# A hybrid scan/attention block with routed experts: a launch with fewer loads, vector-engine norms, late constants, a first pair of batches, and three changes of order and places

## The chip, the cores and the metric

The kernel runs on one core of a Trainium2 chip. The core has a matrix engine (PE), a vector engine (DVE), a scalar engine (ACT), a general engine (POOL), and a sync engine (SP) that mostly issues DMA transfers. Each engine works through its own list of instructions in order and waits on semaphores where it needs another's result. The metric is device time in microseconds (us) of one execution; the number given is the median over the runs.

## The reference

The input x has 8 batches of 512 tokens of width 256, all in float32. Four steps follow each other, each adding to x: a scan layer, a mixture of experts, causal attention, and the same mixture of experts again.

```python
x = x + scan(layernorm(x))        # silu(x @ Win), h = 0.9*h + xt*Bp, y = h.Cp + Dp*xt, y @ Wout
x = x + ffn(layernorm(x))
x = x + attention(layernorm(x))   # 16 heads of width 16, causal, softmax, Wout
x = x + ffn(layernorm(x))
```

Since the scan's state is decayed by one constant and multiplied by Bp and Cp for each channel, the kernel scans one number per channel and multiplies by sum(Bp*Cp). The ffn is

```python
scores = sigmoid(x @ router_w.T)              # 16 experts in 4 groups, best 2 groups, best 4 experts
tw = scores of the 4 chosen / their sum * 2.5
routed = sum over the 4: tw * (silu(x@gate_w) * (x@up_w)) @ down_w
sh = silu(x @ sh_gate_w) * (x @ sh_up_w) @ sh_down_w       # shared experts, every token
return routed + sh
```

## The kernel before

A batch is a tile of 128 partitions by NT = 4 rows of 256 numbers. The program has four stretches of time. The **Scan stage** goes over the 8 batches; then the **routed experts** of the first ffn; then the **Attention stage** over the 8 batches; then the routed experts of the second ffn, beside which the sums of finished batches go to the output.

Inside a stage, `stretch` builds, for every batch b, a set of pieces (Python generators) and `beside` weaves them by how many matmul columns each piece has behind it: `timed(piece, at...)` puts the steps of a piece at given shares of the batch's main work. So the program's order is laid down when the kernel is built, and a scheduler keeps dependences by semaphores; `tc.keep_in_program_order` pins an instruction to the place where it was written, and `tc.issue_after` keeps it behind another one. In loop b of the Scan stage there run: the main work of batch b (`Scan.main`: four times a projection pz, a sigmoid on ACT, the product xi on DVE, the scan on DVE, a multiplication on ACT and the sum y on DVE, then the output projection py and its addition to x); the norm, transposes, logits and choice of experts of batch b-1 (`Route`); the sending of batch b-2's rows to the experts' lists (16 indirect DMAs on POOL, L665); the shared experts of batch b-2; and the loading, norm and transposes of batch b+1. In Scan `ahead` is 1, in Attention 2, where the first two batches are prepared beside the last routed blocks by `prepared`.

`normed` (L376) makes a layernorm: statistics by bn_stats and bn_aggr on DVE, 1/sqrt(var + eps) either by a DVE addition and a pow on POOL (L401, L402), or, with `by_vector`, by an integer first guess and three Newton steps on DVE; then four row normalisations on DVE (L405). For a routed batch its output is the tile sorted_m, of which the iota on POOL (L526) fills the token numbers. The gain write (L651) puts the four weights of each token into that tile; the tile is then sent by the DMAs of L665. The tag "rows" holds two such tiles.

`routed` (L765) works through 136 blocks of 128 rows. `load` (L792) brings a block's rows, in tag "kb4", on SP; `fetch` copies an expert's weights; `turn`, `up` and `down` do the matmuls; a scatter DMA on POOL (L859) adds the results to part 0. The shared experts' output ys_m goes to part 1 by SP (L948). There is a branch (L889, L892) ahead of the blocks for an unlikely overflow; each engine passes it. `load_sum` (L140) loads part 0 and part 1 of a batch and adds them on DVE at one go (L145). In Attention, L991 makes the queries and keys, which L999 to L1002 copy into masked places (`w_all`), half of it on ACT and half on DVE; L1046 makes the scores.

At the head of the program x_0 and x_1 go out on SP, the weights of Scan on ACT, the shared experts' weights sg, su and sd on SP and ACT, and small ones on POOL; the routing's constants (parity, mine, groups, cand_*, below) are made on DVE from the identity.

Of the kernel before, what the change touches and what calls it, by code (L numbers as in the profile page):

```python
# [15 lines left out]
P = 128  # L16
# [7 lines left out]
HG = 4  # L24
# [50 lines left out]
def tile_hybrid_block(  # L75
# [56 lines left out]
    def load_x(b: int):  # L132
        x_sb = xpool.tile([P, NT, D], FP, tag="x", name=f"x_{b}")
        x_tiles[b] = x_sb
        return nc.sync.dma_start(out=x_sb, in_=x_in[b].rearrange("(t p) d -> p t d", p=P))
# [4 lines left out]
    def load_sum(i: int, b: int, more, queue=nc.sync):  # L140

        x_sb = xpool.tile([P, NT, D], FP, tag="x", name=f"x{i}_{b}")
        queue.dma_start(out=x_sb, in_=rows_of(parts[i][0], b))
        queue.dma_start(out=more, in_=rows_of(parts[i][1], b))
        nc.vector.tensor_add(x_sb, x_sb, more)  # L145
        x_tiles[b] = x_sb

# [28 lines left out]

    sg_sb = const.tile([P, KD, NSH * F], FP, name="sg_sb")
    nc.sync.dma_start(out=sg_sb, in_=sh_gate_w.rearrange("(k p) f -> p k f", p=P))
    su_sb = const.tile([P, KD, NSH * F], FP, name="su_sb")
    nc.scalar.dma_start(out=su_sb, in_=sh_up_w.rearrange("(k p) f -> p k f", p=P))  # L180
    sd_sb = const.tile([P, NSH * KF, D], FP, name="sd_sb")
    nc.sync.dma_start(out=sd_sb, in_=sh_down_w.rearrange("(k p) d -> p k d", p=P))
# [32 lines left out]
    nc.gpsimd.memset(decay, DECAY)  # L215
# [3 lines left out]
    nc.vector.tensor_mul(bc_all, bp_sb, cp_sb)  # L219
    bc_sb = const.tile([P, NI], FP, name="bc_sb")  # L220
    nc.vector.tensor_reduce(bc_sb, bc_all, AX.X, ALU.add)

    def load_attention_weights():
# [9 lines left out]
    nc.vector.tensor_reduce(  # L233
        parity, ident.rearrange("p (q w c) -> p w q c", q=HG, w=2), AX.XY, ALU.add
# [29 lines left out]
    nc.vector.tensor_reduce(mine, ident.rearrange("p (g e) -> p e g", e=E), AX.X, ALU.add)  # L264
    groups = const.tile([P, P // E], FP, name="groups")
    nc.vector.tensor_reduce(groups, ident.rearrange("p (g e) -> p g e", e=E), AX.X, ALU.add)
    cand_e = const.tile([P, 1], FP, name="cand_e")
    spelled = const.tile([P, E], FP, name="spelled")
    nc.vector.tensor_mul(spelled, mine, numbers)
    nc.vector.tensor_reduce(cand_e, spelled, AX.X, ALU.add)  # L270
    cand_j = const.tile([P, CAND], FP, name="cand_j")
    nc.vector.tensor_mul(spelled[:, 0 : P // E], groups, numbers[:, 0 : P // E])
    nc.vector.tensor_reduce(cand_j[:, 0:1], spelled[:, 0 : P // E], AX.X, ALU.add)
    for c in range(1, CAND):
        nc.vector.tensor_scalar(cand_j[:, c : c + 1], cand_j[:, 0:1], float(c * (P // E)), None, ALU.add)
    below = const.tile([P, E], FP, name="below")
    nc.vector.tensor_scalar(below, numbers, cand_e, None, ALU.is_lt)
    cand_at = const.tile([P, 2, CAND], FP, name="cand_at")
    nc.vector.tensor_scalar(cand_at[:, 1, :], cand_j, float(BLK), None, ALU.mult)
    for c in range(CAND):  # L280
        nc.vector.tensor_scalar(cand_at[:, 0, c : c + 1], cand_e, float(WEXP), None, ALU.mult)
        nc.vector.scalar_tensor_tensor(
            cand_at[:, 1, c : c + 1], cand_e, float(REG), cand_at[:, 1, c : c + 1], ALU.mult, ALU.add
        )
# [91 lines left out]
    def normed(b: int, tag: str, place, by_vector: bool = False):  # L376

        x_sb = x_tiles[b]
        stats = small.tile([P, NT, 6], FP, tag="stats", name=f"stats_{tag}")
        mv = small.tile([P, NT, 2], FP, tag="mv", name=f"mv_{tag}")  # L380
        for t in range(NT):
            nc.vector.bn_stats(stats[:, t, :], x_sb[:, t, :])
            nc.vector.bn_aggr(mv[:, t, :], stats[:, t, :])
            yield
        rstd = small.tile([P, NT], FP, tag="rstd", name=f"rstd_{tag}")
        if by_vector:


            var = small.tile([P, NT], FP, tag="var", name=f"var_{tag}", bufs=1)
            nc.vector.tensor_scalar(var, mv[:, :, 1], EPS, None, ALU.add)  # L390
            bits = small.tile([P, NT], I32, tag="bits", name=f"bits_{tag}", bufs=1)
            nc.vector.tensor_scalar(bits, var.bitcast(I32), 1, None, ALU.logical_shift_right)
            nc.vector.tensor_scalar(rstd.bitcast(I32), bits, -1.0, HALVED, ALU.mult, ALU.add)
            off = small.tile([P, NT], FP, tag="off", name=f"off_{tag}", bufs=1)
            for _ in range(3):
                nc.vector.tensor_mul(off, rstd, rstd)
                nc.vector.scalar_tensor_tensor(off, off, -0.5, var, ALU.mult, ALU.mult)
                nc.vector.scalar_tensor_tensor(rstd, off, 1.5, rstd, ALU.add, ALU.mult)
            yield
        else:  # L400
            nc.vector.tensor_scalar(rstd, mv[:, :, 1], EPS, None, ALU.add)  # L401
            nc.gpsimd.tensor_tensor(rstd, rstd, neg_half, ALU.pow)  # L402
        xn = place()
        for t in range(NT):
            nc.vector.tensor_scalar(  # L405
                xn[:, t, :], x_sb[:, t, :], mv[:, t, 0:1], rstd[:, t : t + 1], ALU.subtract, ALU.mult
            )
            yield
# [24 lines left out]
    class Scan:  # L433
# [4 lines left out]
        norms, scores, choose = (0.08, 0.2, 0.32, 0.4), (0.48, 0.52, 0.61, 0.66), (0.71, 0.97)  # L438

# [72 lines left out]
    counts = [region, region]  # L512
    upto = {}

    class Route:
# [8 lines left out]
        def place(self):  # L524
            rows = work.tile([P, NT, ROW], FP, tag="rows", name=f"sorted_{self.tag}")
            nc.gpsimd.iota(  # L526
                rows[:, :, D + 2 * TK :].bitcast(I32), [[P, NT], [0, 8]], base=self.b * T, channel_multiplier=1
# [4 lines left out]
        def norm(self, by_vector: bool = False):  # L532
            return normed(self.b, self.tag, self.place, by_vector)
# [27 lines left out]
    def choices(i: int, b: int, tag: str, held, paced: bool):  # L561
# [89 lines left out]
        nc.vector.scalar_tensor_tensor(  # L651
# [113 lines left out]
    def routed(i: int, table, beside):  # L765
# [4 lines left out]
        held = {}  # L770
# [21 lines left out]
        def load(n: int):  # L792
            if n not in held:
                values(n)
            rows = work.tile([P, 4 * D], FP, tag="kb4", name=f"rows_{i}_{n}", bufs=KB)
# [73 lines left out]
        def run(first: int, last: int):  # L869
            load(first)  # L870
# [25 lines left out]
    def shared_experts(i: int, b: int, xnT_of, tanh: bool):  # L896
# [3 lines left out]
        def steps():  # L900
# [47 lines left out]
            nc.sync.dma_start(out=rows_of(parts[i][1], b), in_=y_sb)  # L948
# [15 lines left out]
    class Attention:  # L964
        mixture, ahead, copies = 1, 2, by_both
        early = 2
        norms, scores, choose = (0.0, 0.12, 0.2, 0.28), (0.42, 0.46, 0.55, 0.6), (0.66, 0.95)

# [4 lines left out]
        def load(self, b: int):  # L973
            load_sum(0, b, kb4(f"more0_{b}"))
# [157 lines left out]
    def prepared(b: int):  # L1132
# [17 lines left out]
        def begin():  # L1150
            x_sb = xpool.tile([P, NT, D], FP, tag="x", name=f"x0_{b}")
            more = free_home("v", f"more_{b}")
            for j, dst in ((1, more), (0, x_sb)):
                nc.gpsimd.dma_start(out=dst, in_=rows_of(parts[0][j], b))
            held.update(x=x_sb, more=more)

        def add():
            for t in range(0, NT, 2):
                rows = held["x"][:, t : t + 2, :]
                tc.keep_in_program_order(nc.vector.tensor_add(rows, rows, held["more"][:, t : t + 2, :]))  # L1160
            x_tiles[b] = held["x"]
# [30 lines left out]
    def stretch(layer):  # L1192
# [5 lines left out]
        def norm(b: int):  # L1198
# [4 lines left out]
            return normed(b, f"l{i}_{b}", place)  # L1203

        def turn(b: int):
            return turned(lambda: xn.pop(b), f"l{i}_{b}", lambda xnT: xT.update({b: xnT}), layer.copies)
# [11 lines left out]
        for b in range(layer.ahead):  # L1218
# [4 lines left out]
            else:  # L1223
                layer.load(b)
                issue(Piece(0, norm(b)))
                issue(Piece(0, turn(b)))
            if b == 0:
                issue(project(b))
        def start_route(b: int):
# [4 lines left out]
        for b in range(B):  # L1234
            pieces = [layer.main(b, made.pop(b))]
# [15 lines left out]
            if b > 0:  # L1251
                r = start_route(b - 1)
                if last:
                    pieces.append(timed(r.norm(), *spread(0.0, 0.12, NT), *spread(0.2, 0.28, NT)))
# [15 lines left out]
            if nxt < B:  # L1270
                layer.load(nxt)
# [5 lines left out]
            if layer.ahead == 1 and nxt < B:  # L1277
                issue(project(nxt))
        layer.end()
# [163 lines left out]
```

## Time and profile before

| | us |
|---|---|
| median of 3 runs (1785.84 to 1786.67) | 1786.35 |
| profiled execution | 1778.1 |
| its span | 1776.4 |

Where PE was busy in the profiled execution, from the busy time of each engine by stretch:

| stretch, us from the start | length | PE busy | DVE busy | PE clock granted |
|---|---|---|---|---|
| 0 to 20, launch | 20 | 3.95 | 8.59 | 1.00 |
| 20 to 60, first Scan batch | 40 | 32.77 | 33.32 | 0.91 |
| 60 to 120, Scan | 60 | 60.00 | 49.97 | 1.00 |
| 120 to 280, Scan | 160 | 151.80 | 115.10 | 1.00 |
| 280 to 320, end of Scan | 40 | 30.72 | 26.27 | 0.79 |
| 320 to 374, last shared experts | 54 | 48.19 | 23.03 | 0.99 |
| 374 to 780, routed experts | 406 | 405.04 | 231.23 | 0.99 |
| 780 to 800, start of Attention | 20 | 9.96 | 8.70 | 0.74 |
| 800 to 1350, Attention | 550 | 539.48 | 358.28 | 1.00 |
| 1350 to 1360, second routed start | 10 | 4.00 | 2.50 | 0.66 |
| 1360 to the end | 416.4 | 388.82 | 233.45 | 0.97 |

In these tables and in the profile's lines a matmul's busy time ends where the model of the pipeline ends it, "idle before" is the time in which the engine stood before an instruction, and the arrow names what ended that wait. SPq and POOLq are the queues of DMA-issuing instructions of SP and POOL. Batch starts in Scan are taken as the first pz matmul of a batch on PE: 63.87 (batch 2), 102.27 (3), 141.68 (4), 183.40 (5), and 264.82 (7).

### The profile page before, as it was taken

How to read it: one execution, taken by the hardware profiler on the slowest of the kernel's cores; microseconds unless marked ns; L12 is line 12 of the kernel's file. 1: busy time of each engine (PE TensorE's matmuls, PEld its weight loads, DVE VectorE, ACT ScalarE, POOL GpSimd, SP SyncE). 2: the span in 40 equal slices, each digit the busy share in tenths (PEclk: the TensorE clock that was granted, in tenths of full speed). 3: DMA queues.
4: the chain of work that ended last, by engine and by line, in shares of the span. 5: the costliest groups of instructions: out<-in, count | busy, mean ns of one | idle time of the engine just before them, and what ended most of it. 6: DMA issues, size and time to landing. Idle time of an engine off the chain costs nothing. (4 is left out here: it accounts for less than half of the span.)

```text
span 1776.4 us, 32812 instructions
## 1 busy us (share of the span) xinstructions
PE 1674.7 (94%) x10640; PEld 1253.8 (71%) x10640; DVE 1090.5 (61%) x3399; ACT 805.7 (45%) x1740; POOL 772.2 (43%) x675
## 2 busy tenths in 40 slices
PE   5999998989999999979999999999998999999994
PEld 3566664579999999954445455455466999999993
DVE  5977767435555655545776675766753665555552
ACT  2322222135555555535654554544523555555552
POOL 4255554625555655530021422312452555555663
PEclk9999998999999999989999999999999999999997
DMA  5443322535555655530012112112443555566766
GB/s 168 161 152 128 131 91 91 184 76 96 95 98 108 103 98 94 98 83 13 25 50 73 63 61 73 52 58 78 145 177 79 94 98 94 103 134 128 129 123 178
DMA packets 149998, 181.37 MB, mean 102 GB/s; under 512 B 16096, under 2 KB 136960, under 8 KB 149824
## 3 DMA queue, kind: packets, MB, share of 16 engines
q0 software_dynamic: 54432, 81.53, 24.1%
q1 hardware_dynamic: 93600, 93.50, 17.3%
q10 hardware_dynamic: 1792, 4.19, 0.6%
q8 instruction: 89, 1.46, 0.3%
q14 instruction: 85, 0.70, 0.1%
HBM read 81.62 MB, written 97.53 MB: 101 GB/s over the span
## 5 line engine op out<-in xcount | busy, mean ns | idle before, releaser
L859 POOL DMA_INDIRECT part<-rows x272 | 428.3, 1575 | 363.6 <-ACT rows L858 287.4
L665 POOL DMA_INDIRECT xg<-sorted_m,slots_m x256 | 256.5, 1002 | 279.4 <-ACT slots_m L662 115.5
L822 PEld LDWEIGHTS ph<-rows,gate 128*128 128x128 f32 x2176 | 285.9, 192 | 15.8 <-ACT rows L812 1.1
L822 PE MATMUL ph<-rows,gate 128*128 128x128 f32 x2176 | 289.3, 276 | 0.6 <-ACT rows L812 0.6
L822 PE MATMUL ph<-rows,up 128*128 128x128 f32 x2176 | 288.5, 276 | 0.0
L850 PE MATMUL pyr<-w_all,rows 128*128 x1088 | 280.4, 380 | 0.0
L822 PEld LDWEIGHTS ph<-rows,up 128*128 128x128 f32 x2176 | 266.0, 193 | 0.0
L830 ACT ACTIVATE rows<-ph 128x256 f32<-128x256 f32 x272 | 104.5, 384 | 328.7 <-PE ph L822 328.7
L831 DVE TENSOR_TENSOR rows<-ph,rows 128x256 f32<-128x256 f32 x272 | 115.3, 424 | 194.1 <-ACT rows L830 193.8
L850 PEld LDWEIGHTS pyr<-w_all,rows 128*128 128x128 f32 x1088 | 185.2, 191 | 14.2 <-ACT rows L858 0.4
L804 ACT COPY gate<-w_all 128x512 f32 x272 | 170.1, 627 | 14.7 <-SPq L892 2.5
L1057 ACT ACTIVATE w_all<-ps_a 128x1024 f32<-128x1024 f32 x128 | 124.4, 1021 | 80.2 <-PE ps_a L1046 74.1
L804 DVE COPY up<-w_all 128x512 f32 x272 | 119.5, 440 | 33.3 <-PE ph L822 18.1
L858 ACT ACTIVATE rows<-pyr,gain 128x256 f32<-128x256 f32 x272 | 128.6, 473 | 14.4 <-PE pyr L850 12.2
L1046 PE MATMUL ps_a<-w_all 32*128 32x512 f32 (+3 forms) x1024 | 122.1, 472 | 7.1 <-ACT w_all L1057 5.7
L911 PE MATMUL pg_m<-xT_m,su_sb 128*128 128x512 f32 x256 | 126.6, 617 | 0.8 <-DVE sig_m L929 0.8
L835 DVE SCALAR_TENSOR_TENSOR gain<-rows,expert_b 128x4 f32<-128x4 f32 x272 | 61.2, 225 | 103.8 <-ACT rows L858 84.2
L911 PE MATMUL pg_m<-xT_m,sg_sb 128*128 128x512 f32 x256 | 123.0, 603 | 0.0
L939 PE MATMUL pd_m<-sd_sb,act_m 128*128 128x256 f32 x512 | 120.5, 384 | 0.0
L832 DVE TENSOR_TENSOR rows<-ph,rows 128x256 f32<-128x256 f32 x272 | 115.1, 423 | 8.3
L811 PE MATMUL pt<-ident,rows 128*128 128x128 f32 x544 | 105.0, 275 | 13.4 <-DMA rows<-xg 13.1
L939 PEld LDWEIGHTS pd_m<-sd_sb,act_m 128*128 128x128 f32 x512 | 96.1, 191 | 21.1 <-issue 4.7
(219 smaller groups left out, 2203.0 us busy)
## 6 DMA issues: line engine op xcount, KB each, us to landing
rows<-xg SPq DMA_DIRECT2D x272, 136.0 KB, 2.6
part<-x SPq DMA_DIRECT2D x16, 512.0 KB, 3.0
part<-ys_m SPq DMA_DIRECT2D x16, 512.0 KB, 3.0
w_all<-in_L_ffn_gate_w_dram SPq DMA_DIRECT2D x24, 256.0 KB, 5.4
w_all<-in_L_ffn_up_w_dram SPq DMA_DIRECT2D x24, 256.0 KB, 4.8
w_all<-in_L_ffn_down_w_dram SPq DMA_DIRECT2D x24, 256.0 KB, 5.6
sum<-part POOLq DMA_DIRECT2D x10, 512.0 KB, 3.9
xg<-zeros SPq DMA_DIRECT2D x34, 136.0 KB, 2.3
```

Of the source, the lines that this page charges most:

```text
L665: nc.gpsimd.indirect_dma_start(out=xg[i], out_offset=bass.IndirectOffsetOnAxis(ap=slots[:, at : at + 1], axis=0), in_=rows[:, t, :], in_of ...
L804: copy(here, w_all[:, bass.ds(held[n][0] + half * KD * F, KD * F)])
L822: nc.tensor.matmul(ph[:, s, f * P : (f + 1) * P], lhsT=both[s][:, k * F + f * P : k * F + (f + 1) * P], rhs=rows[:, ROW + k * P : ROW + (k ...
L831: nc.vector.tensor_mul(act, ph[:, 0, :], act)
L832: nc.vector.tensor_mul(act, ph[:, 1, :], act)
L850: nc.tensor.matmul(py, lhsT=act[:, f * P : (f + 1) * P], rhs=w_all[:, bass.ds(w + 2 * KD * F + f * D, D)], start=(f == 0), stop=(f == KF - 1),
L858: nc.scalar.mul(rows[:, 0:D], py, gain[:, TK : TK + 1])
L859: nc.gpsimd.indirect_dma_start(out=parts[i][n % 2], out_offset=bass.IndirectOffsetOnAxis(ap=rows[:, D + 2 * TK : D + 2 * TK + 1].bitcast(U ...
L911: nc.tensor.matmul(dst, lhsT=w[:, k, f * P : (f + 1) * P], rhs=xnT[:, k, :], start=(k == 0), stop=(k == KD - 1),)
L939: nc.tensor.matmul(py[:, j, :], lhsT=acts[n][:, f, t * P : (t + 1) * P], rhs=shared[n][3][:, f, :], start=(n == 0 and f == 0), stop=(n == ...
L1046: nc.tensor.matmul(ps[j // 2][:, j % 2, col : col + n], lhsT=k_sb[w][r, o, c * P : (c + 1) * P], rhs=q_sb[r, o, c * P : T], start=True, st ...
L1057: nc.scalar.activation(es[two], ps[two][:, :, 0:cols], AF.Exp, scale=ATT_SCALE)
```

## The change

**Launch.** x_0 comes in four pieces, alternately on SP and ACT; the three loads of the shared experts' weights move behind batch 0's transposes, all on SP; decay is set on DVE, and a sigmoid on it loads ACT's table early. Batches 0 and 1 of Scan take their norm by Newton steps, pinned, and batch 0's transposes are copied by ACT and DVE. The DVE constants are kept in a list: two are issued with batch 1, the rest after batch 2.

**First pair.** `first_two` issues batch 0's four scan steps, batch 1's transposes, batch 1's four scan steps, and then batch 0's output projection; the loop begins at b = 1 with what is left of batch 1.

**Order and places.** In Scan the four row normalisations of batch b are kept behind the gain write of batch b-1, and the iota is pinned, which puts POOL's pow ahead of it; the last batch uses other shares (`last_rows`). The first two blocks of a routed run load into tag "rows", and the last batch's ys_m is written out by POOL. `load_sum` returns its addition as two pinned halves, which Attention puts at shares 0.24 and 0.28 of a batch.

```diff
 def load_x(b: int):
+        if b == 0:
+            for t in range(NT):
+                (nc.scalar if t % 2 else nc.sync).dma_start(out=x_sb[:, t, :], in_=src[:, t, :])
+            return None
...
 def load_sum(i: int, b: int, more, queue=nc.sync):
-        queue.dma_start(out=x_sb, in_=rows_of(parts[i][0], b))
         queue.dma_start(out=more, in_=rows_of(parts[i][1], b))
-        nc.vector.tensor_add(x_sb, x_sb, more)
+        queue.dma_start(out=x_sb, in_=rows_of(parts[i][0], b))
+        def added():
+            for t in range(0, NT, 2):
+                rows = x_sb[:, t : t + 2, :]
+                tc.keep_in_program_order(nc.vector.tensor_add(rows, rows, more[:, t : t + 2, :]))
+                yield
+        return added()
...
+    pending = []
+    def by_vector(op, *args):
+        pending.append(lambda: tc.keep_in_program_order(op(*args)))
...
+    def load_shared():
+        nc.sync.dma_start(out=sg_sb, in_=sh_gate_w.rearrange("(k p) f -> p k f", p=P))
+        nc.sync.dma_start(out=su_sb, in_=sh_up_w.rearrange("(k p) f -> p k f", p=P))
+        nc.sync.dma_start(out=sd_sb, in_=sh_down_w.rearrange("(k p) d -> p k d", p=P))
...
-    nc.gpsimd.memset(decay, DECAY)
+    nc.vector.memset(decay, DECAY)
+    nc.scalar.activation(begun, decay, AF.Sigmoid)
...
 def normed(...):
         for t in range(NT):
-            nc.vector.tensor_scalar(xn[:, t, :], ...)
+            with tc.issue_after(past().ins) if past() is not None else nullcontext():
+                keep(nc.vector.tensor_scalar(xn[:, t, :], ...))
...
 class Route:
-            nc.gpsimd.iota(...)
+            tc.keep_in_program_order(nc.gpsimd.iota(...))
...
+            past = (lambda: gained.get(self.b - 1)) if self.i == 0 else lambda: None
+            return normed(self.b, self.tag, self.place, by_vector, past=past)
...
-        nc.vector.scalar_tensor_tensor(
+        gained[b] = nc.vector.scalar_tensor_tensor(
             rows[:, :, D : D + TK], gain, ROUTE_SCALE, ...
...
 def load(n: int):
+            if n - first_of[0] < 2:
+                rows = work.tile([P, NT, ROW], FP, tag="rows", name=f"rows_{i}_{n}")
+                rows = rows.rearrange("p t c -> p (t c)")[:, 0 : 4 * D]
+            else:
+                rows = work.tile([P, 4 * D], FP, tag="kb4", name=f"rows_{i}_{n}", bufs=KB)
...
-            nc.sync.dma_start(out=rows_of(parts[i][1], b), in_=y_sb)
+            (nc.gpsimd if b == B - 1 else nc.sync).dma_start(out=rows_of(parts[i][1], b), in_=y_sb)
...
+        def first_two():
+            layer.load(1)
+            issue(Piece(0, norm(1, True)))
+            for _ in range(2):
+                pending.pop(0)()
+            main = layer.main(0, made.pop(0))
+            issue(Piece(0, some(main.steps, NI)))
+            issue(Piece(0, turn(1)))
+            issue(project(1))
+            second = layer.main(1, made.pop(1))
+            issue(Piece(0, some(second.steps, NI)))
+            issue(main)
+            return Piece(second.columns - NI * KD * T, second.steps)
...
-        for b in range(B):
-            pieces = [layer.main(b, made.pop(b))]
+        begun = None
+        if layer.mixture == 0:
+            begun = first_two()
+        for b in range(1 if begun else 0, B):
+            pieces = [begun or layer.main(b, made.pop(b))]
...
             if nxt < B:
-                layer.load(nxt)
+                added = layer.load(nxt)
+                if added is not None:
+                    pieces.append(timed(added, 0.24, 0.28))
...
+            if i == 0 and b == 2:
+                for make in pending:
+                    make()
```

## The prediction

> **What bounds the kernel now.** I read the page's busy table first, then the waits of PE, then the timelines of PE, DVE, POOL and SP at each long wait.
>
> ```profile
> PE 1674.7 (94%) x10640; PEld 1253.8 (71%) x10640; DVE 1090.5 (61%) x3399; ACT 805.7 (45%) x1740; POOL 772.2 (43%) x675
> ```
>
> TensorE (PE) sets the pace: 1776.4 - 1674.7 leaves 102 us in which it stood. The change leaves the number of PE instructions as it is, so only this idle time, and the slow clock after it, can be won. The waits of PE say where it lies:
>
> ```profile
> PE pt_l L368 <- DVE xn L405: 16.0, 4, 15.0
> PE pt L811 <- DMA rows<-xg: 13.1, 4, 6.2
> PE py_s L421 <- DVE y_s L482: 9.2, 6, 2.0
> PE pl_m L549 <- ACT xT_m L370: 9.2, 2, 7.5
> PE pt_l L368 <- DVE w_all L1002: 8.6, 1, 8.6
> PE pt_m L368 <- DVE sorted_m L405: 3.9, 2, 2.1
> ```
>
> That is the launch, the two starts of the routed experts, the Scan batches, Scan's last batch, and the start of Attention. The timelines name what each waits for. The launch (DVE, then PE):
>
> ```profile
> 10.40 0.43 DVE L382 BATCH_NORM_STATS2 stats_l<-x 128x6 f32<-128x256 f32 x1 [2.00 <-DMA x<-in_L_attn_a_x_dram]
> 14.58 0.41 DVE L405 TENSOR_SCALAR xn<-x,mv_l,rstd_l 128x256 f32<-128x256 f32 x1
> 15.04 0.69 PE L368 MATMUL pt_l<-ident,xn 128*128 128x128 f32 x2 [15.04 <-DVE xn L405]
> 18.54 8.50 PE L466 MATMUL pz_s<-xT_l,w_scan 128*128 128x512 f32 x16 [0.25 <-ACT xT_l L370]
> ```
>
> x_0's statistics were done at 8.4, but DVE stood at x_1's first, then did constants (12.33 to 14.51). Inside Scan (batch 4, which starts on PE at 141.68; POOL, then DVE):
>
> ```profile
> 149.09 0.16 POOL L526 IOTA sorted_m<- 128x32 int32 x1 [2.71 <-PE pr_m L616]
> 149.23 1.04 POOL L402 TENSOR_TENSOR rstd_m<-rstd_m,neg_half 128x4 f32<-128x4 f32 x1
> 150.31 1.38 DVE L405 TENSOR_SCALAR sorted_m<-x,mv_m,rstd_m 128x256 f32<-128x256 f32 x4 [8.19 <-POOL rstd_m L402]
> 151.61 0.75 DVE L476 SCALAR_TENSOR_TENSOR xi_s<-pz_s,b_in_sb,xi_s 128x512 f32<-128x512 f32 x1
> ```
>
> DVE's next task, xi_0, needs nothing of POOL, but stands behind four sorted rows whose rstd is behind an iota that waits for old gather DMAs. The start of Attention (PE, then DVE):
>
> ```profile
> 779.45 0.60 PE L368 MATMUL pt_l<-ident,early 128*128 128x128 f32 x4
> 788.67 1.11 PE L368 MATMUL pt_l<-ident,early 128*128 128x128 f32 x4 [8.61 <-DVE w_all L1002]
> 786.72 1.23 DVE L145 TENSOR_TENSOR x<-x,more 128x1024 f32<-128x1024 f32 x1 [12.48 <-DMA more<-part]
> 787.87 0.75 DVE L1002 TENSOR_SCALAR w_all<-pq_a,parity 128x512 f32<-128x512 f32 x1
> ```
>
> The copy that PE needs (L1002) was ready at about 777 (ACT's half of the same copy began at 776.20), but stood behind batch 2's addition, whose operands had not landed. And a routed start (SP, PE):
>
> ```profile
> 368.97 0.38 SPq L948 DMA_DIRECT2D part<-ys_m  x1
> 372.07 2.59 SPq L796 DMA_DIRECT2D rows<-xg  x4
> 374.44 0.66 PE L811 MATMUL pt<-ident,rows 128*128 128x128 f32 x2 [6.12 <-DMA rows<-xg]
> ```
>
> [...] L1002 starts 0.07 us before the addition's end (787.95), and no earlier. [...] 0.52 granted in 314.8 to 316.8 after 2.06 us of idle, 0.50 in 788.6 to 791.8. So a gap costs more than its length. [...] fewer loads ahead of it can help. The trace: 330 to 416 GB/s between 3.3 and 7 us, while x_0, W_in and shared weights moved together. [...] the trace has 1.28 at 19.00, behind the first pz, so preloading it is worth nothing.
>
> **The change part by part.** All sums are against the profiled execution: 1778.1 us, span 1776.4. The median shown is 1786.35, 8.25 above it; I carry the same difference over.
>
> *Launch and paired batches.* x_0 in four pieces lands at an estimated 4.9 instead of 6.65 (three 512 KB transfers no longer share the rate; both ends 4.4 and 6.2). Statistics are done about 6.5. Twelve Newton operations at 0.16 to 0.20 cost 2.3, where add and POOL pow took 1.3 (10.74 to 12.03), but nothing stands between: xn_0 at 8.8 instead of 14.58, first pz about 12.1 instead of 18.54. The pairing then makes PE wait about 3 for xn_1 (20.6 to 23.6, DVE has batch 0's scan first) and about 4.4 for sorted_m_0 (DVE reaches it at 47.7 to 49.3 after two scans of 4 x (0.74 + 1.22 + 0.75)). Batch 2 starts at about 56.5 instead of 63.87: **-7.4** (-3 to -9). Late constants, 2.3 of DVE, land before batch 3.
>
> *Batches 2 and 3.* Batch 2 took 38.4 without a PE wait and with DVE full. DVE now enters it with a backlog (xi_0 5.5 after its start) and sorted_m_1 after gain_0: PE stalls about **+3.0** (0 to +5). Batch 3: the constants and a little stall, **+0.5** (-1 to +2).
>
> *Batches 4 to 6* took 41.7 each. xi_0 can start 2.65 after the batch's start (ACT's sigmoid) instead of 9.9. From xi_0 (151.61) to the gain write (163.65) DVE worked almost without a break, so the gain comes about S+16.1, the four sorted rows, spaced between xi_3, the scan and y_3, S+16.75 to 19.2. PE wants them at S+17.6 (159.29 - 141.68): about 1.4 of stall comes new; the y_s wait 1.75, the sig_m wait 0.85 and the clock loss go. About 39.8 each, as in batch 3: **-5.7** for three (-8 to 0).
>
> *Batch 7.* DVE's 7.25 wait for rstd_m (272.44) goes; sorted_m_6 is done about 282.6, the two ACT copies take 1.07, so logits start at about 284.2 instead of 286.45: **-2.2** (-3.5 to -1). sorted_m_7 waited until 314.30 for the landing of sorted_m_5's gather, whose 16 DMAs (1.27 each on POOL) began after gain_5 at 285.61. Now gain_5 is at about 279.5, the landing about 7 earlier: PE's 2.06 idle and the slow clock behind it (8 transposes 2.00 instead of 0.87, 16 matmuls 4.17 instead of 3.45) go: **-3.9** (-4 to -1).
>
> *Routed starts.* SP no longer waits for ys_7, and the second block's tile no longer waits for that buffer. But the semaphore values in the built program show that the first row load waits for POOL's branch bookkeeping, and POOL issues ys_7 ahead of it, after ACT's copy (ends 368.95). POOL's direct DMA takes 0.59 to 1.18 (the sum<-part rows), the branch lines about 1.2 (SP's own took 1.19 and 1.13 at the second start): load at 371.2 to 371.7 instead of 372.07. **-0.5** each, **-1.0** in both (-3 to +2).
>
> *Attention.* In the new order of DVE both L1002 copies come first and batch 2's two half additions (0.68 each as against one of 1.23) come after some twelve mask operations, past 790, where the operands landed at 786.7. PE's 8.61 goes; transposes, scores and projection right after, 5.67 at half clock, take 3.7; ACT's table load and exp then give a little back. The scores end at 781.8 instead of 791.8; I take **-9.5** (-10.5 to -6). In later batches DVE no longer stands about 3 us at an addition; PE did not wait there: 0 (-1.5 to +1.5).
>
> *Sum:* -7.4 + 3.0 + 0.5 - 5.7 - 2.2 - 3.9 - 1.0 - 9.5 = **-26.2**. Profiled 1751.9, median 1760.1.
>
> **Rivals.**
> *A, the starts give what they seem to offer.* If POOL gets through early, the loads go out when SP is free, and each start wins 3.0 more: -6 more, 1754. For: SP's wait was only for ys_7. Against: the semaphore order above.
> *B, Scan gives it back.* The sorted rows, now behind the gain, make PE wait in batches 4 to 7 as long as y_s did, and -5.7 and -2.2 go, the pair costs 5: about 1770. For: DVE is nearly full for S+2.65 to S+19. Against: the continuous DVE run above.
> *C, the Attention gap stays:* another operand of the copy or PSUM bank holds PE; 1769.6. Against: ACT's half of the same product ran at 776.20.
> *D, slower.* The gain write is set not by DVE's order but by the choices' own chain (PE sums, POOL), and stays at S+22 (163.65 - 141.68). The rows then end at about S+24.5, 7 after PE wants them, with about 1 of slow clock, in batches 2 to 7: 6 x 8 = 48, less the 5.7 + 2.2 that also fail to come: -26.2 + 7.9 + 48 - 3.5 (already counted) = +26, 1812. It decides against the change from about 5 per batch. Against it: choices feeding that write come from logits of the batch before, and DVE's only other wait between 150 and 164 is 0.2 us, on ACT.
> That the change does nothing would need DVE's order to be unlike the built program's.
>
> **How the numbers follow.** Forecast 0.58, A 0.15, B 0.15, C 0.07, D 0.05. The forecast's terms have their own spread of about 8 either way; with A below and B and C above, 1749 to 1772 leaves out about 2 in 10. About 0.2% (3.6 us) is what a measurement of this kernel can tell from no change. Faster by more: the first four cases, 0.95, less their far ends, 0.94; slower: D less its near end, 0.04; within 0.2%: the rest, 0.02.
>
> **What would show it.** First transpose at about 9.5 and first pz near 12; a PE wait for xn_1 and sorted_m_0 between 20 and 50; batches 4 to 6 at about 39.8 with DVE's wait for rstd_m gone; no wait of PE at 314; PE waits of 5.5 to 6 left before both routed stages; no wait for L1002's copy at the start of Attention and under 2 us idle there. PE waits for sorted_m of over 5 us in each Scan batch would prove it wrong, as would a standing gap before the first scores.

## The result, and the profile after

The changed kernel takes 1769.51 us, median of 4 runs (1766.56 to 1770.22); the kernel before, beside it, 1786.14. The ratio is 0.9901, 95% interval 0.9888 to 0.9914. The profiled execution took 1766.56, span 1764.9, so between the two profiled executions the gain is 11.5, between the medians 16.6. The profiled execution of the kernel before was a quick one: its 1778.1 lies below every one of 24 later runs of the same kernel (1780.72 to 1791.55). What follows counts in profiles of single executions; a second pair of profiles, towards the end of the next section, shows which of these figures repeat.

PE is still the bound (the page's busy table), and the list of its waits has changed places (PE's waits; total, times, longest):

```profile
PE 1678.5 (95%) x10640; PEld 1255.2 (71%) x10640; DVE 1097.8 (62%) x3429; ACT 806.3 (46%) x1739; POOL 773.4 (44%) x674
```

```profile
PE pt L853 <- DMA rows<-xg: 14.8, 7, 5.8
PE pt_l L394 <- DVE xn L434: 13.1, 4, 9.8
PE pt_m L394 <- DVE sorted_m L434: 12.6, 9, 3.3
PE ps_a L1091 <- ACT w_all L1102: 5.4, 11, 1.0
PE pz_s L497 <- ACT xT_l L396: 2.4, 1, 2.4
```

The waits for y_s, for the logits' copy of 7.5 and for the second query copy are gone. PE waits for sorted_m nine times instead of twice, and both routed starts stay. In Scan's last batch the logits wait 0.46 where they had waited 7.51, and the last eight transposes of sorted rows run at one go without a wait (PE's timeline):

```profile
279.69 0.61 PE L586 MATMUL pl_m<-rw_sb,xT_m 128*128 128x16 f32 x2 [0.46 <-ACT xT_m L396]
306.24 1.04 PE L394 MATMUL pt_m<-ident,sorted_m 128*128 128x128 f32 x8
```

The launch and the first pair on PE's timeline, and two stretches of the busy times (length, then PE, PEld, DVE, ACT, POOL, then the granted clock):

```profile
9.84 2.20 PE L394 MATMUL pt_l<-ident,xn 128*128 128x128 f32 x8 [9.84 <-DVE xn L434]
11.87 8.18 PE L497 MATMUL pz_s<-xT_l,w_scan 128*128 128x512 f32 x16
22.72 0.76 PE L394 MATMUL pt_l<-ident,xn 128*128 128x128 f32 x4 [2.68 <-DVE xn L434]
27.60 8.84 PE L497 MATMUL pz_s<-xT_l,w_scan 128*128 128x512 f32 x16 [2.40 <-ACT xT_l L396]
49.12 0.47 PE L394 MATMUL pt_m<-ident,sorted_m 128*128 128x128 f32 x1 [3.19 <-DVE sorted_m L434]
```

```profile
25.00:30.00 5.00, 2.60 (x4) 1.17 (x4) 4.41 (x7) 2.10 (x4) 0.71 (x2) 0.50 0.00 0
50.00:55.00 5.00, 5.00 (x19) 3.93 (x17) 3.17 (x7) 1.17 (x2) 2.14 (x3) 0.50 0.68 219
```

PE stands three times, 2.68, 2.40 and 3.19. The granted clock was still 1.00 from 22 to 24, then 0.56 from 24 to 26 and 0.50 up to 30, so the second gap fell into half clock; after the third it was 0.50 again (50 to 55). In batch 4 of Scan, POOL's pow now comes ahead of the iota, DVE starts on xi_0 at once, and the sorted rows follow the gain write (POOL, then DVE, then PE):

```profile
141.28 1.04 POOL L429 TENSOR_TENSOR rstd_m<-rstd_m,neg_half 128x4 f32<-128x4 f32 x1 [0.28 <-DVE rstd_l L428]
143.92 0.16 POOL L559 IOTA sorted_m<- 128x32 int32 x1 [1.60 <-DMA xg<-sorted_m,slots_m]
143.40 0.75 DVE L507 SCALAR_TENSOR_TENSOR xi_s<-pz_s,b_in_sb,xi_s 128x512 f32<-128x512 f32 x1 [2.20 <-ACT xi_s L506]
156.24 0.17 DVE L688 SCALAR_TENSOR_TENSOR sorted_m<-choices_sm,den_m 128x16 f32<-128x16 f32 x1
157.58 0.41 DVE L434 TENSOR_SCALAR sorted_m<-x,mv_m,rstd_m 128x256 f32<-128x256 f32 x1
159.48 0.97 PE L394 MATMUL pt_m<-ident,sorted_m 128*128 128x128 f32 x3 [0.84 <-DVE sorted_m L434]
```

At the start of Attention PE runs through (PE's timeline); the eight early transposes stand together, where 8.61 us had parted them:

```profile
769.53 1.04 PE L394 MATMUL pt_l<-ident,early 128*128 128x128 f32 x8
770.49 1.14 PE L1091 MATMUL ps_a<-w_all 32*128 32x512 f32 x8
```

The first routed start (POOL, SP, PE), and the increment by which POOL closes its branch, from the source view of its branch line (shortest/median/longest in ns, then when):

```profile
358.79 0.92 POOL L992 DMA_DIRECT2D part<-ys_m  x1 [10.51 <-ACT ys_m L990]
361.30 4.99 SPq L838 DMA_DIRECT2D rows<-xg  x7
363.66 0.66 PE L853 MATMUL pt<-ident,rows 128*128 128x128 f32 x2 [5.79 <-DMA rows<-xg]
```

```profile
L935 POOLq INC_SWDGE_SEM  x1: 1002/1002/1002, 360.1 to 360.1; - x1
```

SP's first row load goes out 0.2 us after that increment ends. Set side by side, the two profiles give this account (us; the last column is what the stage added to the difference):

| mark on PE | before | after | stage |
|---|---|---|---|
| batch 2's first pz | 63.87 | 59.98 | -3.89 |
| batch 3's | 102.27 | 100.87 | +2.49 |
| batch 4's | 141.68 | 140.76 | +0.48 |
| batch 7's | 264.82 | 260.41 | -3.49 |
| batch 7's logits | 286.45 | 279.69 | -2.35 |
| end of Scan's shared experts | 368.32 | 357.87 | -3.69 |
| first routed block | 374.44 | 363.66 | -0.33 |
| Attention's first queries | 769.13 | 759.21 | +0.86 |
| end of the first eight score records | 791.80 | 771.63 | -10.25 |
| end of Attention's shared experts | 1349.66 | 1331.47 | +1.98 |
| second routed block run starts | 1355.88 | 1336.70 | -0.99 |
| PE's last matmul ends | 1749.80 | 1735.06 | +4.44 |
| end of the span | 1776.4 | 1764.9 | +3.24 |

At the second routed start the changed kernel is 19.2 ahead; 7.7 of that is given back after it.

### The profile page after: what moved, and what is told of

Its sections match the earlier page's. It is cut to its first block, busy times and chain, and to the rows that moved or that the text cites. A ratio compares the mean times of both kernels' runs of the same rounds, so it can differ in the third digit from the quotient of the medians.

```text
span 1764.9 us, 32859 instructions
## 1 busy us (share of the span) xinstructions
PE 1678.5 (95%) x10640; PEld 1255.2 (71%) x10640; DVE 1097.8 (62%) x3429; ACT 806.3 (46%) x1739; POOL 773.4 (44%) x674
## 5 line engine op out<-in xcount | busy, mean ns | idle before, releaser
L864 PEld LDWEIGHTS ph<-rows,gate 128*128 128x128 f32 x2176 | 286.0, 192 | 16.1 <-ACT rows L854 1.5
```

Source lines behind the costliest of these rows:

```text
L864: nc.tensor.matmul(ph[:, s, f * P : (f + 1) * P], lhsT=both[s][:, k * F + f * P : k * F + (f + 1) * P], rhs=rows[:, ROW + k * P : ROW + (k ...
```

## The experiments

The runs were made in three sets on different chips, each set beside the kernel before, whose medians there were 1785.48, 1784.95 and 1805.60. So versions are compared by their ratio to that kernel, and not by their medians.

**The place of Attention's addition.** The halves stand at the head of each batch instead of at 0.24 and 0.28.

```diff
-                    pieces.append(timed(added, 0.24, 0.28))
+                    for _ in added:
+                        pass
```

> The changed kernel, but Attention's half additions stand at the head of each batch again instead of at shares 0.24 and 0.28. Theory (the addition's place on DVE made the gap at the start of Attention): PE stands 8 to 9 us for the second query copy before the second half of the early transposes, the first four score matmuls end about 20 us after the first transposes instead of about 2, and the whole is 9 to 11 us slower than the changed kernel (1779 to 1780). Rival (the gap went because the loads landed sooner, or by another part): no such wait, and within 2 us of 1769.5.

1766.53 (1766.37 to 1774.92), ratio 0.9909 (0.9879 to 0.9939). The theory's gap did not come (from the first queries to the end of the first score records 12.43 us, as in the changed kernel), but the output projection of Attention's first batch came 48.63 after that mark, not 44.34. In the built order the pinned halves had slid behind both query copies and the transposed copy, and there DVE stood 5.23 us for the landing. So this edit did not restore the old place, and speaks neither for the theory nor for its rival. The next does restore it, with the old unpinned addition at the batch's load:

```diff
-            return load_sum(0, b, kb4(f"more0_{b}"))
+            more = kb4(f"more0_{b}")
+            load_sum(0, b, more)
+            nc.vector.tensor_add(x_tiles[b], x_tiles[b], more)
```

> The changed kernel with Attention's addition in one unpinned piece where the batch's load is issued, as in the kernel before. In DVE's order it stands between the two query copies again (in the earlier trial of the place alone the pinned halves had slid behind both copies and behind the transposed copy). Theory (what counts is whether the addition stands ahead of the second query copy): PE stands 8 to 9 us there, and from PE's first query matmul of Attention to the end of the first eight score matmuls pass 21 to 23 us, as in the kernel before (22.7), not 12.4; the whole is 8 to 11 us slower than the changed kernel. Rival (the gap needs the old load order or the old stage before it): 12 to 14 us, and no difference.

1775.30 us; its ratio to the kernel before is 0.9951 (0.9939 to 0.9964) against 0.9901 (0.9888 to 0.9914) for the changed kernel, which is 8.9 us of 1786 and inside the theory's 8 to 11. The gap is back (DVE, then PE), 22.46 us from the first queries to the mark:

```profile
775.32 1.22 DVE L1021 TENSOR_TENSOR x<-x,more 128x1024 f32<-128x1024 f32 x1 [12.27 <-DMA more<-part]
776.47 0.74 DVE L1049 TENSOR_SCALAR w_all<-pq_a,parity 128x512 f32<-128x512 f32 x1
777.26 1.11 PE L394 MATMUL pt_l<-ident,early 128*128 128x128 f32 x4 [8.40 <-DVE w_all L1049]
```

An addition that waits for its operands, one instruction ahead of a copy that waits for nothing, is worth 10.0 us at this mark (22.46 - 12.42).

**The sorted rows behind the gain write.**

```diff
-            past = (lambda: gained.get(self.b - 1)) if self.i == 0 else lambda: None
+            past = lambda: None
```

> The changed kernel, but the sorted row normalisations no longer stand behind the gain write; the iota stays pinned behind POOL's pow. Theory (the rows behind the gain win Scan's later batches and its end): DVE waits for rstd_m again, 5 to 8 us in batches 4 to 6, these batches take 40.7 to 41.7 instead of 39.9, PE waits for the logits' transposed copy in batch 7 and 2 us for the last sorted tile; together 6 to 9 us slower than the changed kernel, though batch 2 gets back up to 2.5. Rival (POOL's pow ahead of the iota is what helps): the waits for rstd_m are under 2 us and the time is within 2 us of 1769.5.

1768.74 (1762.61 to 1773.46), ratio 0.9902 (0.9869 to 0.9934): not parted from the changed kernel, so the theory's 6 to 9 us did not come, and the rival's number did. But DVE still stands, and the trace shows a different reason from the one that I had read before. DVE's waits from 50 to 320 us hold this line, and POOL and DVE in batch 4:

```profile
DVE sorted_m L434 <- DMA xg<-sorted_m,slots_m: 31.6, 6, 7.5
```

```profile
143.29 1.05 POOL L429 TENSOR_TENSOR rstd_m<-rstd_m,neg_half 128x4 f32<-128x4 f32 x1
146.61 0.16 POOL L559 IOTA sorted_m<- 128x32 int32 x1 [2.27 <-DMA xg<-sorted_m,slots_m]
```

```profile
146.60 1.38 DVE L434 TENSOR_SCALAR sorted_m<-x,mv_m,rstd_m 128x256 f32<-128x256 f32 x4 [7.54 <-DMA xg<-sorted_m,slots_m]
```

The pow is done at 144.34, ahead of the iota, and DVE still stands until 146.60: the rows are written into one of two tiles, out of which the gather of two batches earlier is still being read. The kernel before showed the pow as the releaser because it came last there, but its being first changes little; with the rows behind the gain DVE no longer stands here (143.40 above). The batches then took 38.98, 39.38, 41.08, 39.64 and 41.34 (batches 2 to 6) against 40.89 and 39.89 and three of 39.88 to 39.89. PE waited 6.2 in batch 7 for the logits' copy again, and Scan's shared experts ended at 360.17, 2.3 later than in the changed kernel. Summed up, the rule costs 2.42 in batches 2 and 3 and wins 2.41 in batches 4 to 6, nothing over the five; it wins 0.42 more up to batch 7's logits and 1.62 from there to the end of the shared experts. Against the kernel before these last two stages are shorter by 1.93 and 2.07 without the rule too; no run took the pinned iota or the last batch's shares away, so what brought that stays open. To keep only what the rule wins, I put it only there:

```diff
-            past = (lambda: gained.get(self.b - 1)) if self.i == 0 else lambda: None
+            past = (lambda: gained.get(self.b - 1)) if self.i == 0 and self.b > 2 else lambda: None
```

> The changed kernel, but the sorted rows stand behind the gain write only from batch 3's rows on (in loop 4 and later), not in loops 2 and 3. Theory (the rule pays where old gathers are still landing in the tile and costs where DVE is full): batch 2 takes 38.5 to 39.5 instead of 40.9, batch 3 39.2 to 39.9, batches 4 to 6 39.9 as in the changed kernel; 1.5 to 2.5 us faster. Rival (what is won early is lost in the next batch): batch 4 takes over 41 and the sum is the same.

1764.31 (1762.43 to 1765.45), ratio 0.9898 (0.9881 to 0.9914), not parted from 0.9901. Batch 2 took 38.99, but batch 3 41.07, and batches 4 to 6 39.9; batch 4 began 1.35 earlier than in the changed kernel. Two of the three expectations held; batch 3 gave back part, with a granted clock of 0.83 from 120 to 130, in which PE waited 0.54.

**The pairing.**

```diff
-            begun = first_two()
+            for _ in range(2):
+                pending.pop(0)()
```

> The changed kernel without the pairing of batches 0 and 1: the loop begins at batch 0 as before, batch 1's norm uses POOL's pow again; fewer loads, batch 0's Newton norm and the late constants stay. Theory (the pairing costs more than it gives: from the first pz to the start of batch 2 the changed kernel took 48.1, the kernel before 45.3, and batch 2 then 40.9 instead of 38.4): batch 2 starts at 57 to 59 instead of 60.0, batch 3 at 96 to 98 instead of 100.9, the whole 3 to 5 us faster than the changed kernel (about 1765.5). Rival (the pairing hides DVE work that would otherwise stall PE): batch 3 starts at 101 or later, and the whole is the same or slower.

1768.36 (1764.20 to 1771.66), ratio 0.9910 (0.9884 to 0.9936). The rival's signs came: batch 3 starts at 105.69, and the whole is the same. But this did not tell the pairing apart, since the first transpose came at 15.14: on DVE's timeline batch 1's statistics had slid in among batch 0's Newton steps and waited for x_1:

```profile
11.45 0.43 DVE L409 BATCH_NORM_STATS2 stats_l<-x 128x6 f32<-128x256 f32 x1 [5.19 <-DMA x<-in_L_attn_a_x_dram]
```

In the next one they can't, because batch 1's norm is pinned at its own place (this edit on top of the one above):

```diff
-                    timed(norm(nxt), *spread(0.32, 0.44, NT), *spread(0.56, 0.64, NT)),
+                    timed(norm(nxt, i == 0 and nxt == 1), *spread(0.32, 0.44, NT), *spread(0.56, 0.64, NT if i or nxt > 1 else NT + 1)),
```

> The changed kernel without the pairing, but with batch 1's Newton norm pinned at its timed place, so that batch 1's statistics cannot slide ahead of batch 0's first rows (in the first trial without pairing they did, and the first transpose came at 15.1 instead of 9.8). Theory (the pairing itself costs): first transpose at 9.3 to 9.9, batch 2 starts at 57 to 59.5 instead of 60.0, batch 3 at 97 to 99.5 instead of 100.9; 1.5 to 4 us faster than the changed kernel. Rival (the pairing is what makes the early launch worth something): batch 2 starts at 61 or later, no gain or a loss.

The theory falls. 1772.68 us, ratio 0.9945 (0.9921 to 0.9969). The first pz is as early as in the changed kernel (11.88), but batch 1's is at 44.56, not 27.60, and batch 2 begins at 70.60, not 59.98:

```profile
36.95 0.80 PE L394 MATMUL pt_l<-ident,xn 128*128 128x128 f32 x2 [4.42 <-DVE xn L434]
44.56 7.03 PE L497 MATMUL pz_s<-xT_l,w_scan 128*128 128x512 f32 x16
```

Batch 1's pinned norm stands behind all of batch 0's scan on DVE. Without the pairing batch 2 begins at 65.75 or 70.60, by where batch 1's norm stands, in both cases later than the 63.87 of the kernel before. In these two versions the early launch did not reach batch 2; in the changed kernel, with the pairing and with batch 1's norm woven into batch 0's scan, 3.9 us of it did. The two runs don't part the pairing from the place of that norm: no version without the pairing had the norm early.

**The routed starts.** First ACT writes the last shared output instead of POOL:

```diff
-            (nc.gpsimd if b == B - 1 else nc.sync).dma_start(out=rows_of(parts[i][1], b), in_=y_sb)
+            (nc.scalar if b == B - 1 else nc.sync).dma_start(out=rows_of(parts[i][1], b), in_=y_sb)
```

> The changed kernel, but the last batch's shared experts' output is written out by ACT's queue instead of POOL's. Theory (POOL's chain, 0.92 for that DMA, its branch lines and its semaphore increment of 1.00, holds the first row load until 2.8 us after ACT's copy): the load goes out 1.5 to 2 us earlier after PE's end, PE waits 3.8 to 4.3 instead of 5.8 and 5.2 at the two routed starts, 2 to 4 us in all. Rival (SP's or PE's own branch lines set it): waits of 5.2 to 5.8 as before, no change.

1765.76 (1762.20 to 1766.34), ratio 0.9883 (0.9862 to 0.9903), not parted from the changed kernel. PE waited 4.84 and 4.80 at the starts, 0.95 and 0.43 less, where 1 to 2 were expected. The load now went out at 359.65; that ACT's branch lines, behind its own store, held it until then is my reading. Then the store is kept back and issued by SP behind the first two row loads:

```diff
-            (nc.gpsimd if b == B - 1 else nc.sync).dma_start(out=rows_of(parts[i][1], b), in_=y_sb)
+            if b == B - 1:
+                late_store.append(lambda: nc.sync.dma_start(out=rows_of(parts[i][1], b), in_=y_sb))
+            else:
+                nc.sync.dma_start(out=rows_of(parts[i][1], b), in_=y_sb)
...
             load(first + 1)
+            if first == 0:
+                late_store.pop()()
```

> The changed kernel, but the last batch's shared experts' output is written by SP behind the first two row loads of the routed run. Theory (the queue that has the store ahead of its branch bookkeeping sets the first load: POOL's in the changed kernel, ACT's when the store was put there, with PE waits of 4.8): now only ACT's copy and branch are left, the load goes out about 1.6 after PE's last shared matmul, PE waits 4.0 to 4.5 at each routed start instead of 5.8 and 5.2, 2 to 3 us in all. Rival (the landing of the last gather DMAs or the row tiles hold the load): waits of 4.8 or more.

1759.94 (1757.31 to 1764.48), ratio 0.9869 (0.9852 to 0.9885): the one version whose interval lies wholly below that of the changed kernel's first runs (0.9888 to 0.9914). SP and PE at the first start:

```profile
360.29 1.62 SPq L839 DMA_DIRECT2D rows<-xg  x2
362.02 0.38 SPq L996 DMA_DIRECT2D part<-ys_m  x1
```

```profile
362.94 0.41 PE L854 MATMUL pt<-ident,rows 128*128 128x128 f32 x2 [3.84 <-DMA rows<-xg]
```

PE ended at 359.10, the load went out 1.19 later, and the waits are 3.84 and 3.25, less than foreseen. What the traces show of this edit is 1.95 + 1.98 = 3.9 at the two starts. The ratios lie 0.0032 apart, which is 5.7 us; the rest is not explained, the more so as this version's second routed run was 1.6 longer (400.0 against 398.4).

**What is left open: the second routed run.** Both kernels again, for second profiles.

> The kernel before once more, for a second profile of it. From the first block of the second routed run to PE's end its first profile took 393.9 us, and all profiles of changed kernels took 395.1 to 400.4. Theory (that first profile was a quick one; this run's length varies with how the row loads meet the scatters and early sums): 396 to 400 here, a span over 1779. Rival (the changed kernels lose about 4 us there): again 393 to 395.

> The changed kernel once more, beside the others of this call: 1766 to 1771; the second routed run 395 to 400 long, batch starts in Scan within 0.3 us of the first profile [...].

These and the next two are the third set: the kernel before took 1805.60 there and, again, 1804.34. The changed kernel took 1784.10, ratio 0.9878 (0.9835 to 0.9921). PE's second routed run took 395.8 in the kernel before (393.9 the first time) and 398.6 in the changed one (398.4), with PE waits for row loads of 1.8 (0.5) and 3.4 (3.4). The versions above range from 395.1 to 400.4, the two below took 404.1 and 405.7. Neither expectation held cleanly.

The second pair of profiles lies 21.0 apart. Stage by stage, with the marks of the table above:

| stage | first pair | second pair |
|---|---|---|
| to batch 2's first pz | -3.89 | -7.30 |
| batches 2 and 3 | +2.97 | +3.83 |
| batches 4 to 6 | -3.49 | -3.24 |
| to batch 7's logits | -2.35 | -2.31 |
| to the end of Scan's shared experts | -3.69 | -0.95 |
| first routed start, and routed experts | +0.53 | -0.05 |
| start of Attention | -10.25 | -10.58 |
| rest of Attention | +1.98 | -4.99 |
| second routed start | -0.99 | -0.95 |
| second routed run | +4.44 | +2.77 |
| from PE's last matmul to the end | +3.24 | +2.77 |

The start of Attention, batches 4 to 6, the logits and the second routed start repeat. Three stages don't, by 2.7 to 7 us: the launch and pair, the last shared experts, and the rest of Attention. For the first of them the reason can be seen. The third gap, 3.19 and 3.20 long, was followed by a granted clock of 0.50 (50 to 55) in the first profile of the changed kernel; four matmuls behind it took 2.04 there and 1.11 in the second (PE; the four matmuls, first profile, then gap and matmuls of the second):

```profile
53.07 2.04 PE L451 MATMUL py_s<-w_scan,y_s 128*128 128x256 f32 x4
49.37 0.33 PE L394 MATMUL pt_m<-ident,sorted_m 128*128 128x128 f32 x1 [3.20 <-DVE sorted_m L434]
51.82 1.11 PE L451 MATMUL py_s<-w_scan,y_s 128*128 128x256 f32 x4
```

Batch 2 began at 57.79 there instead of 59.98. It then took 42.64 instead of 40.89, so batch 3 began only 0.44 earlier.

In the changed kernel's first profile the waits of the second routed run come after POOL's early loads of a finished batch's sums (POOL, then PE):

```profile
1605.83 0.59 POOL L1392 DMA_DIRECT2D sum<-part  x1 [2.49 <-DMA part<-rows]
1611.39 0.59 POOL L1392 DMA_DIRECT2D sum<-part  x1 [2.56 <-DMA part<-rows]
1612.29 1.59 POOL L901 DMA_INDIRECT part<-rows  x1 [0.31 <-ACT gate L846]
```

```profile
1618.51 0.41 PE L853 MATMUL pt<-ident,rows 128*128 128x128 f32 x2 [1.83 <-DMA rows<-xg]
```

The sum loads wait on POOL for scatters to land (2.49 and 2.56 above), later scatters stand behind them, and SP's row loads wait for scatters (12.3 in four waits between 1606 and 1624). This is read from the trace; no run took the early sums away, and the kernel before has the same early loads, after much the same waits (2.44 to 2.96 for five of its first eight). In the changed kernel's second profile the longest wait stands at the same place, 281.6 after the start of the run (281.8 in the first), and took 2.18. Whether the change itself lengthens this run and the end behind it by some 3 us each, or two profiles of the kernel before are too few, stays open.

**The two gains together, and a shorter pair.** The first is the late store with the rule from batch 3's rows on (both edits above). In the second DVE also finishes batch 1's norm before batch 0's scan, and the two constants issued with batch 1 go ahead of that norm:

```diff
-                    nc.vector.scalar_tensor_tensor(xi, pz, bias, xi, ALU.add, ALU.mult)
+                    with tc.issue_after(normed_last["l0_1"].ins) if b == 0 else nullcontext():
+                        nc.vector.scalar_tensor_tensor(xi, pz, bias, xi, ALU.add, ALU.mult)
```

> The changed kernel with SP's late store behind the first row loads and with the gain rule only from batch 3's rows on. If the two gains stand in different places they add: PE waits 3.3 to 4.0 at the routed starts, batch 4 starts 1.0 to 1.6 earlier, 1757 to 1762. Rival (the second gives back what it wins): the same as the late store alone, 1760.

> The same, and DVE finishes batch 1's norm before it starts on batch 0's scan steps (in the changed kernel the Newton steps were woven between three of them, xn_1 ended at 24.4 and PE stood three times at half clock after). Theory (DVE's order sets batches 0 and 1, since DVE is full from 12 to 47 us): xn_1 ends at about 20, the last scan sum of batch 1 at about 41.5 instead of 43.8, batch 2 starts at 57 to 58.5 instead of 60; 1.5 to 2.5 us less than the version without it. Rival (ACT's transposed copies, behind the sigmoids that wait for scan buffers, set it): batch 1's pz stays at 27 or later and batch 2 at 59.5 or later.

Ratios 0.9874 (0.9836 to 0.9913) and 0.9886 (0.9853 to 0.9919), beside 0.9878 for the changed kernel in the same runs: no difference can be told. The first had batch 4 start at 138.54 against 140.32, but waited 6.9 for row loads in the second routed run, against 3.4; the second 9.2. The late store's shorter waits at the routed starts repeat (4.02 and 3.23, 3.75 and 3.16). In the second, batch 1's pz stayed late (28.92, after 7.6 of waiting for ACT's copy) while batch 2 began at 58.79, inside the spread of its neighbours (57.79 for the changed kernel, 60.12 for the first combination): inconclusive. So the late store shortens the two starts in every version that has it, but no version was shown to be faster than the changed kernel in the same set.

## Why the prediction was right, and where it was not

It was right in direction, and 1769.5 lies in its range of 1749 to 1772; but the size was 16.6 where -26.2, or 1760.1, was forecast. The mechanism was right where most of the gain lies, at the start of Attention. Most of its terms came out near what was worked: the first pz (12.1 forecast, 11.87), batches 2 and 3 (+3.5, +2.97), batch 7's logits (-2.2, -2.35), the last sorted tile (-3.9, -3.69), the routed starts (-1.0, -1.32) and Attention's start (-9.5, -10.25). Of the rivals, A fell at the starts, for the reason that the prediction gave: POOL's branch lines behind its store (0.92 for the store, 1.00 for the increment that closes the branch); the late store shows that part of A's gain is to be had. B fell for batches 4 to 6, C and D altogether (no wait at the start of Attention; the gain write came at 156.24, 15.48 after the batch's start, where 16.1 was forecast). That B's 1770 and C's 1769.6 lie nearer to what came than the forecast does is chance: neither's waits are there.

Three of the terms that fit are in part luck. The first pz is the sum of two misses: DVE was through with the statistics at 5.83, not 6.5, and the Newton steps took 2.9 (5.87 to 8.79), not 2.3. The logits and the last sorted tile were put down to the new order of rows, and of -2.35 and -3.69 the rule accounts for 0.42 and 1.62 by the run without it.

Three terms were mis-sized, and one was missing.

- **The launch and the pair**, -7.4: it measured -3.89. The launch itself was 6.67 earlier at the first pz; the pair then lost 2.8 of it. The prediction priced the two gaps but not the slow clock behind them, which it had itself named as dearer than a gap's length. Batch 1's 16 pz matmuls took 8.84 with a granted clock of 0.50 until 30; the same 16 took 7.03 without pairing (44.56, above). And a further gap of 2.40, priced at nothing, came from ACT: its transposed copies (26.97) stood behind a sigmoid that had waited 3.46 until DVE's delayed y was done. How much of this counts was not the same in both profiles: in the second pair, with 1.11 instead of 2.04 for the four matmuls behind the last gap, the term came out at -7.30, and up to batch 4's start the change won 3.47, against 0.92 in the first pair and a forecast of 3.9. ACT's table load, 1.28 long in both (at 19.00 before, at 2.80 after), won nothing by its new place, as forecast: before, ACT still waited 1.65 for the first pz behind it.
- **Batches 4 to 6**, -5.7: measured -3.49. They took 39.88 to 39.89, as forecast (39.8), but I took 41.7 for all three before, and only batch 4 took that; 5 and 6 took 40.72 and 40.70, which the starts 183.40, 224.12 and 264.82 show.
- **Attention after its start**, 0: measured +1.98. About 1.8 of that is clock: in its last batch a gap of 1.01 before the same scores was followed by a granted clock of 1.00 before (1240 to 1250) and by 0.73 and 0.58 after (1220 to 1225, 1225 to 1230). It is not a cost of the change: from that gap to the logits the kernel before took 21.54 and, in its second profile, 23.09, the changed one 23.34 and 23.48.
- **Everything after the second routed start** was taken to move along unchanged: +7.7 between the profiles, and +5.5 in the second pair. The row waits account for 2.9 of the 7.7 (3.4 against 0.5). The end from PE's last matmul took 29.8 against 26.6, and the second time 32.2 against 29.4; the cause of this was not found. The prediction carried a profile's difference over to the median, and the profile it started from was 8 us under its median, the one after only 3; so the medians moved 5 more than the profiles.

My reading of DVE's 8.19 us wait in batch 4 was the one causal claim that the runs mended: the wait was for the tile, not for the pow alone. The forecast held there because the change moved the rows and not only the pow; and what that won in batches 4 to 6 it had cost in batches 2 and 3, as the forecast's two terms of +3.5 and -5.7 half foresaw.

## What to carry to other kernels

Look, ahead of every long wait of the bounding engine, for an instruction on another engine's list that waits while the next one could run; moving it a few places was worth 10 us here, and an edit that aims at the same place must be looked up in the built order, since a scheduler may slide it. When a wait is removed, ask what else the same instruction waits for: the named releaser is only the one that came last (DVE's 8.19 us were put down to POOL's pow; with the pow done first DVE stood 7.54 for the gather). Price each new gap of the matrix engine with the slow clock that can stand behind it, as a chance and not as a fixed cost (2.04 or 1.11 for the same four matmuls here); take a second pair of profiles before a stage's figure is believed, since three stages moved by 2.7 to 7 us here; and follow a semaphore chain through the branch bookkeeping of every engine that has work queued before it (POOL's closing increment alone took 1.00 us here).

## What the hardware showed that was not expected

- **The same gap did not cost the same.** In Scan's first pair a gap of 3.19 us was followed by a granted clock of 0.50 (50 to 55) and four matmuls in 2.04 us in one profile of the changed kernel, and a gap of 3.20 by the same four in 1.11 us in the other; batch 2 began 2.19 us apart. A gap of 1.01 us in Attention was followed by a granted clock of 1.00 in the first profile of the kernel before (1240 to 1250) and by 0.73 and 0.58 in the first of the changed one (1220 to 1225, 1225 to 1230). In the two profiles of the kernel before, the same 12 score matmuls behind this gap took 2.52 and 3.60. What sets the clock behind a gap was not shown.
- **The branch took longer on POOL than on ACT.** POOL's closing increment took 1.00 us alone at the first routed start and 0.65 at the second, where ACT was through its whole branch about 0.5 us after its last copy (358.49 to 359.0, first start). With a store of 0.92 ahead of POOL's branch SP's first row load went out 3.43 us after PE's end (361.30 after 357.87), and with the store behind the loads 1.19 after it.
- **x_0 in four pieces, with less beside it, let DVE start early.** DVE started on the first quarter of x_0 at 3.61 and on the fourth at 5.22, standing nowhere between them for a load; loaded whole, beside other loads, it had held DVE until 6.65. From 3.3 to 7 us the DMA moved 367 GB/s before and 269 after. No run parts the pieces from the fewer loads.
